# Two of the seven block additions of a fast matrix product moved from VectorE into TensorE's PSUM accumulation

## The chip, the cores and the metric

The kernel runs on one core of one Trainium2 chip. The metric is device time in microseconds (us) of one execution. A core has five engines that work side by side and hand over by semaphores: TensorE (PE in the profile, its weight loads PEld), VectorE (DVE), ScalarE (ACT), GpSimd (POOL) and SyncE (SP). TensorE writes only into PSUM, here eight banks of 512 float32 numbers for each of 128 partitions. VectorE and ScalarE read PSUM[...].

## The reference

A macaron block on 4 x 2048 tokens of width 256: half a mixture-of-experts layer, attention, and half a mixture-of-experts layer again, each on a layer norm and with a residual. Everything is float32.

```python
x = x + 0.5 * ffn(layernorm(x))      # 8 experts, top 2, capacity 1.25
x = x + attn(layernorm(x))
x = x + 0.5 * ffn(layernorm(x))

def ffn(x):                          # what matters here
    capacity = int(1.25 * N / E)     # 1280 rows for each of 8 experts
    disp = ...                       # each expert's rows, gathered
    g = einsum("ecd,edf->ecf", disp, wg)      # d = 256, f = 1024
    u = einsum("ecd,edf->ecf", disp, wu)
    eo = einsum("ecf,efd->ecd", silu(g) * u, wd)
    ...                              # weighted and added back to the rows
```

## The kernel before

The two mixture layers are two calls of `experts`. The 1280 rows of an expert are worked in two **units** of 640 rows (`chunks`, five tiles of 128 rows), so a layer has 16 units and the kernel 32. `k` is the unit's number within its layer. A unit has two stages: gate and up (`steps_of`), then the down projection (L680) with the scatter of its rows.

**Gate and up.** The products with `wg` and `wu` are made by a seven-product scheme for 2 x 2 blocks (Strassen in Winograd's form): the width 256 is split into two halves of 128, the rows into two halves of BH = 320, the outputs f into two halves of 512. Sums of weight blocks (`ws`, `sums_of_w`) are made once for an expert, sums of row blocks (`xs`, `sums_of_x`) once for a unit, by VectorE. A unit has NF = 4 **blocks**, p = 0 to 3, of 128 output columns in each half. A block makes seven products, each a pair of matmuls of 128 x 128 by 128 x 320, m = 0 for gate and m = 1 for up. In the order of the code they are: the *first* (`first_product`, weights block 11 with row block 11), the *second* (`p2`), the *third* (into `u2`, L577), the *sixth* (into `ct[:, 3]`, L578), the *fourth* (into `ct[:, 2]`, L580), the *fifth* (`p5`, L583) and the *seventh* (into `ct[:, 1]`, L590). Seven additions on VectorE, all recorded on the helper's line L487, put them together in `ct`, which holds four quarters of gate and up. Then ScalarE takes SiLU of the gate quarters (L563) and the product of gate and up goes to `h` (L566): on GpSimd in one piece for p < 3, on VectorE in two pieces for the last block, where ScalarE works a quarter at a time.

**PSUM.** `banks()` (L515) gives a buffer `mm` of two banks, three of them in turn; `both` fills one with a pair, gate in the first bank and up in the second. The first product alone is made in a single-bank buffer `one` (L547), gate and up at different places of the order, and ScalarE copies each half to `p1` in SBUF (L551), since two additions need it. The seventh and eighth bank are `one` and `tr` (transposes). The down projection's sums also take `banks()`.

**Order.** In `experts` the order on TensorE, VectorE and ScalarE is the order of the source (`tc.manual_schedule(engines=ENGINES - {Pool})`); GpSimd's is planned by the framework, and SyncE only issues large loads. Each engine works its own list in order, and the framework adds the semaphore waits that the tiles' readers and writers need. Between blocks, `beside(k, p)` puts in work for the next unit: after block 1 ScalarE masks three gathered row tiles (`blank`, L470), after block 2 two more; after blocks 2 and 3 TensorE transposes row tiles (L481), which ScalarE copies out (L484). During the down projection `behind(k, i)` adds the remaining transposes, the row and weight sums, the list of the next expert's rows, and the gathers on GpSimd's queue.

The first unit of a layer (k = 0) starts before all its rows have come: its first and second products need only the first 320 rows, and `rest_of_first` (L517) masks, transposes and sums the rest before the third.

Of the kernel before, what the change touches and what calls it, by code (L numbers as in the profile page):

```python
# [8 lines left out]
F32 = mybir.dt.float32  # L9
# [3 lines left out]
AF = mybir.ActivationFunctionType  # L13
ALU = mybir.AluOpType
# [4 lines left out]
P = 128  # L19
# [7 lines left out]
def macaron_kernel(  # L27
# [22 lines left out]
    nc = tc.nc  # L50
# [9 lines left out]
    BANK = 512  # L60
# [374 lines left out]
    BH = CH * P // 2  # L435
    TURN = 3

    def experts(name, src, dst, wait_for, weights, wpool, pool, ppool):
# [23 lines left out]
        def blank(k, *tiles):  # L462
            for i in tiles:
                if k < len(chunks):
                    e, r = chunks[k][0], got[k][i]
                    has = r[:, D + E + e : D + E + e + 1]
                    if k == 0 and i % 2:
                        nc.vector.tensor_scalar(r[:, 0:D], r[:, 0:D], has, None, ALU.mult)
                    else:
                        nc.scalar.mul(r[:, 0:D], r[:, 0:D], has)  # L470

        def turn(k, q):

            if k >= len(chunks):
                return
            if q == 0:
                turned[k] = xTs[k] = pool.tile([P, DC, CH * P], F32, tag="xsT", name="xsT", bufs=2)
            c, i0, i1 = q // 2, (0, TURN)[q % 2], (TURN, CH)[q % 2]
            ps = ppool.tile([P, BANK], F32, tag="tr", name="tr", bufs=1)
            for i in range(i0, i1):  # L480
                nc.tensor.transpose(  # L481
                    ps[:, (i - i0) * P : (i - i0 + 1) * P], got[k][i][:, c * P : (c + 1) * P], ident
                )
            nc.scalar.copy(turned[k][:, c, i0 * P : i1 * P], ps[:, : (i1 - i0) * P])  # L484

        def tt(o, a, b, op):
            nc.vector.tensor_tensor(o, a, b, op)  # L487
# [14 lines left out]
        def sums_of_x(k):  # L502
            if k >= len(chunks):
                return
            v = turned.pop(k)
            o = xs[k] = pool.tile([P, 4, BH], F32, tag="xs", name="xs", bufs=1)
            b11, b12, b21, b22 = v[:, 0, :BH], v[:, 0, BH:], v[:, 1, :BH], v[:, 1, BH:]
            tt(o[:, 0, :], b12, b11, ALU.subtract)
            tt(o[:, 1, :], b22, o[:, 0, :], ALU.subtract)
            tt(o[:, 2, :], b22, b12, ALU.subtract)  # L510
            tt(o[:, 3, :], b21, o[:, 1, :], ALU.subtract)

        def banks():

            return ppool.tile([P, 2, BANK], F32, tag="mm", name="mm", bufs=3)  # L515

        def rest_of_first():  # L517

            blank(0, *range(TURN, CH))
            for q in (1, 3):  # L520
                turn(0, q)
            sums_of_x(0)

        def steps_of(k):
            e = chunks[k][0]
            xT, hs = xTs.pop(k), []

            def product(p, m, ps, j, c, b):

                if c is None:  # L530
                    a = ws[e][:, m, j, p * P : (p + 1) * P]
                else:
                    a = weights[e][m][:, c, j * FH + p * P : j * FH + (p + 1) * P]
                nc.tensor.matmul(ps, a, b, start=True, stop=True)  # L534

            def both(p, *what):
                ps = banks()
                for m in range(2):
                    product(p, m, ps[:, m, :BH], *what)
                return ps[:, :, :BH]  # L540

            p1 = {}

            def first_product(p, m):
                if p == NF:
                    return
                one = ppool.tile([P, BANK], F32, tag="one", name="one", bufs=1)  # L547
                product(p, m, one[:, :BH], 0, 0, xT[:, 0, :BH])
                if m == 0:
                    p1[p] = pool.tile([P, 2, BH], F32, tag="p1", name="p1", bufs=2)  # L550
                nc.scalar.copy(p1[p][:, m, :], one[:, :BH])  # L551

            first_product(0, 0)
            for p in range(NF):
                last = p == NF - 1

                ct = pool.tile([P, 4, 2, BH], F32, tag="ct", name="ct", bufs=2)
                u2 = pool.tile([P, 2, BH], F32, tag="u2", name="u2", bufs=1)
                h = pool.tile([P, 2, CH * P], F32, tag="h", name="h", bufs=NF)
                hq = h.rearrange("p j (t s) -> p (j t) s", t=2)  # L560

                def silu(qs):
                    nc.scalar.activation(ct[:, qs, 0, :], ct[:, qs, 0, :], AF.Silu)  # L563

                def finish(engine, qs):
                    engine.tensor_tensor(hq[:, qs, :], ct[:, qs, 0, :], ct[:, qs, 1, :], ALU.mult)  # L566

                p2 = both(p, 0, 1, xT[:, 1, :BH])
                if p == 0:
                    first_product(0, 1)  # L570
                    if k == 0:
                        rest_of_first()
                    x4 = xs.pop(k)
                tt(ct[:, 0], p1[p], p2, ALU.add)
                if last:
                    silu(slice(0, 1))
                tt(u2, p1.pop(p), both(p, 1, None, x4[:, 1, :]), ALU.add)  # L577
                tt(ct[:, 3], u2, both(p, 2, None, x4[:, 2, :]), ALU.add)  # L578
                first_product(p + 1, 0)
                tt(ct[:, 2], ct[:, 3], both(p, 1, 1, x4[:, 3, :]), ALU.add)  # L580
                if last:
                    silu(slice(2, 3))
                p5 = both(p, 0, None, x4[:, 0, :])  # L583
                tt(ct[:, 1], u2, p5, ALU.add)
                tt(ct[:, 3], ct[:, 3], p5, ALU.add)
                first_product(p + 1, 1)
                if last:
                    silu(slice(3, 4))
                    finish(nc.vector, slice(0, 4, 2))
                tt(ct[:, 1], ct[:, 1], both(p, 3, None, xT[:, 1, BH:]), ALU.add)  # L590
                if last:
                    silu(slice(1, 2))
                    finish(nc.vector, slice(1, 4, 2))
                else:
                    silu(slice(0, 4))
                    finish(nc.gpsimd, slice(0, 4))
                hs.append(h)
                yield hs
# [54 lines left out]
        first = following[0]  # L653
        with tc.manual_schedule(engines=ENGINES - {mybir.EngineType.Pool}):
# [14 lines left out]
            for k, (e, i0) in enumerate(chunks):  # L669
                for p, hs in enumerate(steps_of(k)):  # L670
                    beside(k, p)
# [4 lines left out]
                for i, p, j in order:  # L676
                    if i not in po:
# [4 lines left out]
                        start=(p == 0 and j == 0), stop=(p == NF - 1 and j == 1),  # L682
# [399 lines left out]
    with tc.tile_pool(name="w1", bufs=2) as wpool:  # L1082
        weights = {}
        with tc.tile_pool(name="r1", bufs=1) as pool, tc.tile_pool(name="r1p", bufs=2, space=PSUM) as ppool:
# [5 lines left out]
            with tc.manual_schedule(engines=ENGINES):  # L1090
                nc.gpsimd.memset(wrx, 0.0)
                ps = ppool.tile([P, DC, P], F32, tag="turn", name="wrT", bufs=1)
# [4 lines left out]
                ps = ppool.tile([P, DC, P], F32, tag="turn", name="means", bufs=1)  # L1097
# [74 lines left out]
```

## Time and profile before

| what | value |
|---|---|
| time, median of 3 runs | 2045.0 us (2043.48 to 2046.27) |
| the profiled execution | 2038.74 us, its span 2036.9 us, mean granted clock of TensorE 0.959 |
| TensorE busy (PE) | 1875.8 us, 92% |
| weight loads (PEld) | 1440.3 us, 71% |
| VectorE busy | 1417.6 us, 70% |
| ScalarE busy | 657.1 us, 32% |
| GpSimd busy | 883.1 us, 43% |
| additions of products on VectorE (L487 with `mm`) | 896, some 820 ns each |
| ScalarE copies of the first product (L551) | 256, 427 ns each |
| SiLU on ScalarE (L563) | 224, 1.27 us for 1280 elements, 0.47 us for 320 |

A page gives busy time by engine, the span in 40 slices, and groups of instructions by line with the mean length of one and the idle time of its engine before them. A float32 matmul of the source stands as two matmul instructions and two weight loads. Records of successive matmuls overlap[...].

The two mixture layers stand at about 105 to 914 us and 1213 to 2037 us of the span; the attention lies between them, and a router with little work for TensorE ahead of each layer.

### The profile page before, as it was taken

The page shows a single profiled execution, that of the slowest core. Times are in us where ns is not written, and L with a number is a line of the kernel's source. Part 1 is how long each engine was busy: PE and PEld are TensorE (multiplying, and loading weights), DVE is VectorE, ACT ScalarE, POOL GpSimd, SP SyncE. Part 2 cuts the span into 40 slices and gives each one's busy share as a digit, 9 for nine tenths or more (in the row PEclk, how much of TensorE's full clock was granted, in tenths as well). Part 3 has the DMA queues.
Part 4 walks back from the last instruction along what each step waited for, and adds up shares of the span by engine and source line. Part 5 has one row for each costly group of instructions (what it writes and reads, how often), then busy time and mean ns, then how long its engine had stood idle before and what let it go on. Part 6 is the DMA issues. An engine that isn't in the chain of part 4 may idle for free.

```text
span 2036.9 us, 24719 instructions
## 1 busy us (share of the span) xinstructions
PE 1875.8 (92%) x9176; PEld 1440.3 (71%) x9176; DVE 1417.6 (70%) x2531; ACT 657.1 (32%) x1325; POOL 883.1 (43%) x737
## 2 busy tenths in 40 slices
PE   6379999999999999998999528999999999999998
PEld 4247777777777777777887415777777777777776
DVE  8867676767676767546798886767676676767654
ACT  5322323232223223225565403232222222232221
POOL 5335353535353535335555303535353535353533
PEclk8589999999999999999999858999999999999999
DMA  9902222223131322115002631313232313131211
GB/s 349 302 28 38 78 40 77 57 59 78 38 80 37 79 40 41 17 16 171 32 32 86 206 111 28 79 37 79 39 82 37 82 37 82 35 85 34 43 14 14
DMA packets 99928, 147.63 MB, mean 72 GB/s; under 512 B 7512, under 2 KB 86368, under 8 KB 99680
## 3 DMA queue, kind: packets, MB, share of 16 engines
q1 hardware_dynamic: 69072, 102.77, 15.0%
q0 software_dynamic: 30720, 43.27, 12.9%
q8 instruction: 73, 1.20, 0.3%
q14 instruction: 47, 0.39, 0.1%
q10 hardware_dynamic: 16, 0.01, 0.0%
HBM read 98.84 MB, written 55.57 MB: 76 GB/s over the span
## 4 chain that ended last, share of the span: by engine, by line
PE 83%; DVE 5%; issue 4%; ACT 1%; POOL 1%; DMA 1%; POOLq 0%; DVEq 0%; ACTq 0%; SPq 0%
PE mm L534 41%; PE mm L680 27%; PE one L534 7%; PE tr L481 2%; PE qp L804 1%; PE pc L859 1%; PE ix L404 1%; PE py L917 1%; DVE st L929 1%; DVE xw L927 1%; DVE q L812 1%; DVE m L817 0%; DVE z L826 0%; DVE st L788 0%; PE trq L847 0%
## 5 line engine op out<-in xcount | busy, mean ns | idle before, releaser
L680 PE MATMUL mm<-wdt,h 128*128 128x256 f32 x2560 | 579.0, 381 | 0.0
L680 PEld LDWEIGHTS mm<-wdt,h 128*128 128x128 f32 x2560 | 475.9, 190 | 63.9
L566 POOL TENSOR_TENSOR h<-ct 128x1280 f32<-128x1280 f32 x96 | 279.0, 2906 | 420.2 <-ACT ct L563 417.6
L534 PE MATMUL mm<-xs,ws 128*128 128x320 f32 x1536 | 456.9, 434 | 2.0 <-DVE xs L487 2.0
L534 PEld LDWEIGHTS mm<-xs,ws 128*128 128x128 f32 x1536 | 292.6, 191 | 124.3 <-DVE xs L487 2.5
L487 DVE TENSOR_TENSOR ct<-ct,mm 128x640 f32<-128x640 f32 x384 | 314.4, 819 | 89.4 <-PE mm L534 83.4
L487 DVE TENSOR_TENSOR ct<-p,mm 128x640 f32<-128x640 f32 x128 | 105.1, 821 | 243.4 <-ACT p L551 200.5
L563 ACT ACTIVATE ct<-ct 128x320 f32<-128x320 f32 (+1 forms) x224 | 182.2, 814 | 278.5 <-DVE ct L487 278.5
L487 DVE TENSOR_TENSOR ct<-u,mm 128x640 f32<-128x640 f32 x256 | 210.3, 822 | 61.1 <-PE mm L534 58.0
L551 ACT COPY p<-one 128x320 f32<-128x320 f32 x256 | 109.3, 427 | 405.4 <-PE one L534 404.4
L690 POOL DMA_INDIRECT out_dram<-eo,ixs x80 | 133.1, 1664 | 220.7 <-ACT eo L689 213.7
L690 POOL DMA_INDIRECT acc<-eo,ixs x80 | 132.8, 1660 | 221.2 <-ACT eo L689 214.2
L456 POOL DMA_INDIRECT r<-rows,ixs x160 | 159.0, 994 | 145.0 <-issue 106.5
L689 ACT ACTIVATE eo<-mm,r 128x256 f32<-128x256 f32 x160 | 76.2, 476 | 396.0 <-PE mm L680 396.0
L534 PE MATMUL mm<-xsT,ws 128*128 128x320 f32 x512 | 158.7, 432 | 0.0
L395 DVE TENSOR_TENSOR lo<-count,slot_lo 128x1024 f16<-128x1024 int16 x112 | 128.3, 1220 | 0.0
L534 PEld LDWEIGHTS mm<-xsT,ws 128*128 128x128 f32 x512 | 97.3, 190 | 40.5
L487 DVE TENSOR_TENSOR u<-p,mm 128x640 f32<-128x640 f32 x128 | 104.9, 820 | 17.0 <-PE mm L534 17.0
L534 PE MATMUL mm<-xsT,wgt 128*128 128x320 f32 x256 | 91.0, 437 | 0.0
L534 PE MATMUL one<-xsT,wgt 128*128 128x320 f32 x256 | 91.0, 437 | 0.0
L534 PE MATMUL mm<-xsT,wut 128*128 128x320 f32 x256 | 90.4, 435 | 0.0
L534 PE MATMUL one<-xsT,wut 128*128 128x320 f32 x256 | 89.9, 433 | 0.0
(209 smaller groups left out, 2316.4 us busy)
## 6 DMA issues: line engine op xcount, KB each, us to landing
wgt<-in_L_ffn_wg_dram SPq DMA_DIRECT2D x16, 1024.0 KB, 4.9
wut<-in_L_ffn_wu_dram SPq DMA_DIRECT2D x16, 1024.0 KB, 6.9
wdt<-in_L_ffn_wd_dram SPq DMA_DIRECT2D x16, 1024.0 KB, 5.5
rows<-xw SPq DMA_DIRECT2D x7, 2176.0 KB, 11.8
xw<-in_L_attn_x_dram SPq DMA_DIRECT2D x16, 512.0 KB, 8.8
out_dram<-xw SPq DMA_DIRECT2D x16, 512.0 KB, 2.9
xw<-acc SPq DMA_DIRECT2D x15, 512.0 KB, 8.7
r<-rows,ixs POOLq DMA_INDIRECT x160, 2.8
```

The source lines that it names most:

```text
L395: nc.vector.tensor_tensor(lo, spread(count.unsqueeze(1), shape), spread(at.unsqueeze(2), shape), ALU.is_equal)
L404: nc.tensor.matmul(self.ps[q, :], self.hv[:, t, :, :], lo[:, t % TG, :], start=(t < Q), stop=(t >= T - Q),)
L456: nc.gpsimd.indirect_dma_start(out=r, out_offset=None, in_=src[:, :], in_offset=bass.IndirectOffsetOnAxis(ap=lists[e][:, i : i + 1], axis=0),)
L481: nc.tensor.transpose(ps[:, (i - i0) * P : (i - i0 + 1) * P], got[k][i][:, c * P : (c + 1) * P], ident)
L487: nc.vector.tensor_tensor(o, a, b, op)
L534: nc.tensor.matmul(ps, a, b, start=True, stop=True)
L551: nc.scalar.copy(p1[p][:, m, :], one[:, :BH])
L563: nc.scalar.activation(ct[:, qs, 0, :], ct[:, qs, 0, :], AF.Silu)
L566: engine.tensor_tensor(hq[:, qs, :], ct[:, qs, 0, :], ct[:, qs, 1, :], ALU.mult)
L680: nc.tensor.matmul(po[i], hs[p][:, j, i * P : (i + 1) * P], weights[e][2][:, j * NF + p, :], start=(p == 0 and j == 0), stop=(p == NF - 1 ...
L689: nc.scalar.mul(eo, po[i], got[k][i][:, D + e : D + e + 1])
L690: ins = nc.gpsimd.indirect_dma_start(out=dst[:, :], out_offset=bass.IndirectOffsetOnAxis(ap=lists[e][:, i0 + i : i0 + i + 1], axis=0), in_ ...
```

## The change

Two additions go into TensorE's accumulation. A matmul with `start=False` adds to what stands in its banks in place of overwriting it.

- The first product's pair is now made in one two-bank buffer of `banks()`, gate and up one after the other, each followed by its copy to `p1`. The second product is then added onto it in the same banks (`onto`, `second_product`), and ScalarE takes the sum out directly: SiLU of the gate half into `ct[:, 0, 0]`, a copy of the up half into `ct[:, 0, 1]`. The addition into `ct[:, 0]` is gone, in all blocks.
- In blocks 0 to 2 the seventh product is added onto the fifth in the fifth's banks, after VectorE has read the fifth for `ct[:, 3]`. One addition makes `ct[:, 1]` from `u2` and the sum. The last block keeps its two additions.
- The first product of block p + 1 stands between the fifth and the seventh of block p. In block 0 the first product stands at the beginning of the unit and, for k > 0, the second behind the third. For k = 0 the second product stands ahead of `rest_of_first`, and with it ScalarE's SiLU.
- The SiLU at the end of blocks 0 to 2 takes three quarters (960 elements) in place of four. The buffer `one` is left to the row lists.

So a block's order on TensorE for p > 0 becomes: second, third, sixth, fourth, fifth, first of the next block, seventh.

```diff
@@ -525,13 +525,14 @@
             e = chunks[k][0]
             xT, hs = xTs.pop(k), []
 
-            def product(p, m, ps, j, c, b):
+            def product(p, m, ps, j, c, b, start=True):
+
 
                 if c is None:
                     a = ws[e][:, m, j, p * P : (p + 1) * P]
                 else:
                     a = weights[e][m][:, c, j * FH + p * P : j * FH + (p + 1) * P]
-                nc.tensor.matmul(ps, a, b, start=True, stop=True)
+                nc.tensor.matmul(ps, a, b, start=start, stop=True, skip_group_check=not start)
 
             def both(p, *what):
                 ps = banks()
@@ -539,18 +540,24 @@
                     product(p, m, ps[:, m, :BH], *what)
                 return ps[:, :, :BH]
 
-            p1 = {}
-
-            def first_product(p, m):
+            first = {}
+
+            def first_product(p):
+
                 if p == NF:
                     return
-                one = ppool.tile([P, BANK], F32, tag="one", name="one", bufs=1)
-                product(p, m, one[:, :BH], 0, 0, xT[:, 0, :BH])
-                if m == 0:
-                    p1[p] = pool.tile([P, 2, BH], F32, tag="p1", name="p1", bufs=2)
-                nc.scalar.copy(p1[p][:, m, :], one[:, :BH])
-
-            first_product(0, 0)
+                ps = first[p] = banks()
+                p1 = pool.tile([P, 2, BH], F32, tag="p1", name="p1", bufs=2)
+                for m in range(2):
+                    product(p, m, ps[:, m, :BH], 0, 0, xT[:, 0, :BH])
+                    nc.scalar.copy(p1[:, m, :], ps[:, m, :BH])
+                first[p] = ps, p1
+
+            def onto(p, ps, *what):
+                for m in range(2):
+                    product(p, m, ps[:, m, :BH], *what, start=False)
+                return ps[:, :, :BH]
+
             for p in range(NF):
                 last = p == NF - 1
 
@@ -565,34 +572,41 @@
                 def finish(engine, qs):
                     engine.tensor_tensor(hq[:, qs, :], ct[:, qs, 0, :], ct[:, qs, 1, :], ALU.mult)
 
-                p2 = both(p, 0, 1, xT[:, 1, :BH])
+                def second_product(ps):
+                    c11 = onto(p, ps, 0, 1, xT[:, 1, :BH])
+                    nc.scalar.activation(ct[:, 0, 0, :], c11[:, 0, :], AF.Silu)
+                    nc.scalar.copy(ct[:, 0, 1, :], c11[:, 1, :])
+
                 if p == 0:
-                    first_product(0, 1)
-                    if k == 0:
-                        rest_of_first()
+                    first_product(0)
+                ps, p1 = first.pop(p)
+                if k == 0 and p == 0:
+                    second_product(ps)
+                    rest_of_first()
+                elif p > 0:
+                    second_product(ps)
+                if p == 0:
                     x4 = xs.pop(k)
-                tt(ct[:, 0], p1[p], p2, ALU.add)
-                if last:
-                    silu(slice(0, 1))
-                tt(u2, p1.pop(p), both(p, 1, None, x4[:, 1, :]), ALU.add)
+                tt(u2, p1, both(p, 1, None, x4[:, 1, :]), ALU.add)
+                if p == 0 and k > 0:
+                    second_product(ps)
                 tt(ct[:, 3], u2, both(p, 2, None, x4[:, 2, :]), ALU.add)
-                first_product(p + 1, 0)
                 tt(ct[:, 2], ct[:, 3], both(p, 1, 1, x4[:, 3, :]), ALU.add)
                 if last:
                     silu(slice(2, 3))
                 p5 = both(p, 0, None, x4[:, 0, :])
-                tt(ct[:, 1], u2, p5, ALU.add)
                 tt(ct[:, 3], ct[:, 3], p5, ALU.add)
-                first_product(p + 1, 1)
                 if last:
+                    tt(ct[:, 1], u2, p5, ALU.add)
                     silu(slice(3, 4))
                     finish(nc.vector, slice(0, 4, 2))
-                tt(ct[:, 1], ct[:, 1], both(p, 3, None, xT[:, 1, BH:]), ALU.add)
-                if last:
+                    tt(ct[:, 1], ct[:, 1], both(p, 3, None, xT[:, 1, BH:]), ALU.add)
                     silu(slice(1, 2))
                     finish(nc.vector, slice(1, 4, 2))
                 else:
-                    silu(slice(0, 4))
+                    first_product(p + 1)
+                    tt(ct[:, 1], u2, onto(p, p5, 3, None, xT[:, 1, BH:]), ALU.add)
+                    silu(slice(1, 4))
                     finish(nc.gpsimd, slice(0, 4))
                 hs.append(h)
                 yield hs
```

## The prediction

> **What bounds the kernel now.** I read the stage table first (busy time of each engine in stretches of 50 us, columns PE, PEld, DVE, ACT, POOL, granted clock, DMA share, GB/s). One row of each kind:
>
> ```profile
> 0.00:50.00 50.00, 30.62 (x406) 24.19 (x406) 40.66 (x147) 26.51 (x70) 29.55 (x66) 0.89 1.01 337
> ...
> 700.00:750.00 50.00, 50.00 (x209) 38.40 (x208) 31.78 (x44) 15.33 (x31) 19.33 (x10) 1.00 0.31 79
> 750.00:800.00 50.00, 50.00 (x266) 37.57 (x265) 37.46 (x47) 15.04 (x30) 25.56 (x18) 1.00 0.21 39
> ...
> 1150.00:1200.00 50.00, 6.46 (x61) 4.55 (x62) 42.77 (x192) 10.41 (x22) 4.29 (x12) 0.55 0.63 218
> ```
>
> From 150 to 900 us and from 1250 to 2000 us every row has PE busy 50.00 of 50 at clock 1.00. These are the two feed-forward stages, where the whole change lies. VectorE is busy 32 to 38 of 50 there, ScalarE about 15. A busy matmul row can hide waiting, so I checked the groups and the timeline:
>
> ```profile
> L534 PE MATMUL mm<-xs,ws 128*128 128x320 f32 x1536 | 456.9, 434 | 2.0 <-DVE xs L487 2.0
> L487 DVE TENSOR_TENSOR ct<-ct,mm 128x640 f32<-128x640 f32 x384 | 314.4, 819 | 89.4 <-PE mm L534 83.4
> L551 ACT COPY p<-one 128x320 f32<-128x320 f32 x256 | 109.3, 427 | 405.4 <-PE one L534 404.4
> ```
>
> ```profile
> 738.80 2.32 PE L534 MATMUL mm<-xs,ws 128*128 128x320 f32 x8
> 740.95 0.70 PE L534 MATMUL one<-xsT,wgt 128*128 128x320 f32 x2
> 741.49 0.70 PE L534 MATMUL mm<-xs,wgt 128*128 128x320 f32 x2
> 742.03 0.70 PE L534 MATMUL mm<-xs,wut 128*128 128x320 f32 x2
> ```
>
> The last column of the groups is idle time before them: 2.0 us in 1536 matmul instructions, while VectorE and ScalarE wait for the matmuls. In the timeline (start, length, engine) one matmul of the source is two instructions and starts 0.54 us after the one before, always. A block p has 14, so 14 x 0.54 = 7.5 us; its seven additions take 7 x 0.82 = 5.7 us beside it. TensorE alone sets the pace, without slack.
>
> **What the Trainium skill says.** "PSUM — Partial Sum Buffer", section "PSUM bank collisions raise a hardware error", wants semaphores by bank and quadrant: two engines may work in different banks at once. The trace agrees: VectorE reads one pair of banks while TensorE fills the next. So no hardware rule makes the second matmul of a pair wait for a reader of the first one's bank; only the program's own waits can. "ScalarE: Activation LUTs", section "What ACT_TABLE_LOAD costs", gives 186 ns + 0.833 ns per element, 93 ns overlap of neighbours, and 1283 ns for a table load. The trace has 427 ns for 320 elements (453 by the formula) and 1.28 us for the load, and I use those. "TensorE: Matmul & The Clock Gate", section "What's actually happening", halves the clock only after an idle window of some 3.4 us. The trace has clock 1.00 at 1000 us with PE busy 48.93 of 50, and 0.55 where PE is busy 6.46. I charge nothing for the clock in mid-stage.
>
> **The change part by part.**
>
> *Additions removed.* 7 x 128 = 896 additions become 96 x 5 + 32 x 6 = 672. The 224 that go, some 0.82 us each, take 184 us off VectorE. All of it lies beside matmuls: worth 0, since TensorE's count stays at 14 per block. The POOL product may start a little earlier; nothing waits for it. Its reader, the down projection, starts several us later.
>
> *ScalarE's new work.* 128 times a SiLU (0.47 us) and a copy (0.43 us) out of the product's banks; against it 96 SiLUs shrink from 1280 to 960 elements (1.27 to about 1.00 us, by line through 0.47 at 320) and 32 go. Sum 128 x 0.90 - 96 x 0.27 - 32 x 0.47 = +74 us, ScalarE from 32% to 36%. By itself it costs nothing.
>
> *The pair of first products.* Here I expect the loss. Before, the two matmuls of a first product stand apart, each in its own allocation of `one`, with other products between. Now they stand next to each other in one two-bank buffer, and ScalarE's copy of the first half is recorded between them. In the order of the built program the second matmul of every pair (128 of 128) carries a wait on ScalarE, and by its count it is for the copy of the first half of the same buffer: the reader of one bank holds the writer of the other. TensorE works in order, so everything behind stands too.
>
> Its price from rows of before. A pair `one` starts at 740.95; its copy on ScalarE starts at 741.69, so 0.74 after the start of the matmul, and takes 0.43:
>
> ```profile
> 738.78 1.27 ACT L563 ACTIVATE ct<-ct 128x1280 f32<-128x1280 f32 x1 [1.50 <-DVE ct L487]
> 739.96 1.30 ACT L470 ACTIVATE r<-r 128x256 f32<-128x256 f32 x3
> 741.69 0.43 ACT L551 COPY p<-one 128x320 f32<-128x320 f32 x1 [0.44 <-PE one L534]
> ```
>
> From a release to running matmuls, the start of the stage shows both steps (127.67 + 0.49 = 128.16 against a weight load at 128.22; three instructions take 1.08 us from a standstill and 0.97 in a stream at 133.98):
>
> ```profile
> 127.67 0.49 DVE L487 TENSOR_TENSOR xs<-xsT,xs 128x320 f32<-128x320 f32 x1 [0.41 <-ACT xsT L484]
> ...
> 128.22 1.08 PE L534 MATMUL mm<-xs,ws 128*128 128x320 f32 x3 [0.99 <-DVE xs L487]
> ```
>
> So 0.74 + 0.43 + 0.05 + 0.11 = 1.33 us from the first matmul to the second, where 0.54 would do: 0.79 us lost per pair. Four pairs per unit, 32 units, less the two that open a stage: 126 x 0.79 = **99.5 us**. Bounds: 0.70 and 0.90, so 88 to 113 us. Nothing covers it.
>
> *Seventh product onto the fifth.* It waits until VectorE has read the fifth. That read starts 0.20 after the fifth's slot ends, takes 0.82, and with 0.16 to restart frees TensorE at 1.18; the first-product pair in between takes 1.08 + 0.79 = 1.87. Hidden, 0. Without the stall above it would show 0.10 us, 96 times.
>
> *Second product onto the first.* It waits for the copy of the second half: 0.79 after that half's slot, covered by the 1.08 of the product between them (the seventh; in block 0 the third). 0.
>
> *Banks held longer.* The first product's pair stays taken until ScalarE has read the sum. By the built order the fourth product takes those banks in block 1, due 6 x 0.54 = 3.23 us after the block's second product began; in blocks 0, 2 and 3 it is the fifth (due at 8 x 0.54 = 4.30 in block 2). In block 2 ScalarE does ahead of that: the SiLU of block 1 from 1.12 (0.20 + 0.82 + 0.10 after the seventh) for 1.00 less 0.09 overlap, three maskings of 0.405 apart, SiLU 0.47 less 0.09, copy 0.43; it ends at 4.05, and TensorE runs at 4.21. It fits by 0.09. Block 1 fits by 0.24, block 3 by 0.46. Charged 0; the upper bound is 0.3 us in block 2 of 30 units, 9 us.
>
> *Opening of each stage (k = 0).* Copy, copy, table load, SiLU and copy now stand ahead of the masking of the last gathered rows, on which the x sums and then TensorE wait. Before, the load stood here, off the path:
>
> ```profile
> 134.35 1.28 ACT L563 ACT_TABLE_LOAD   x1
> ```
>
> The masking began at 125.43 in the first stage. Following the chain at the half clock of that stretch (first half copied by 123.40, second by about 124.9, load to 126.2, SiLU and copy to 127.0) it begins 1.5 to 2.2 us later; at most one clock window later still. I take 2 us per stage, **4 us**, bounds 2 and 8. DMA queues, gathers and scatters keep their order: 0.
>
> Sum 99.5 + 4 = +103.5 us. The profiled execution, 2038.74 us (span 2036.9), becomes 2142; it lies 6.3 us under the median of 2045.0, to which I add the same: **2148 us**.
>
> **The rivals.**
> - *Stall absent*: the wait is met before TensorE arrives. Then the seventh's 0.10 x 96 = 10 us and the 4 us of the openings stay: 2059 us. For it: the banks differ. Against it: ScalarE cannot copy before the first matmul has ended, 0.2 us after the second should have begun.
> - *Banks as well*: ScalarE's reading late in blocks 2 and 3, behind maskings, and the row copy adds some 0.8 us in both: 30 x 1.6 = 48 us more, 2196 us. Against it: those blocks take banks that VectorE frees, until the fifth product.
> - *Faster*: VectorE's release of banks paces the stage and the even matmul rows hide it. The 184 us of additions would then be worth up to all of themselves, 1861 us at the lowest. It decides once a block's VectorE work exceeds 7.5 us; it is 5.7, and VectorE is the one that waits (89.4 us before one group). The same cause at a tiny size would give no change.
>
> **Numbers.** A measurement of this kernel tells about 0.2%, 4 us, from no change. Stall as worked out: 0.86; banks as well: 0.06; stall absent: 0.04 (slower too); VectorE pacing: 0.02 faster, and 0.02 no change. So slower 0.96, same 0.02, faster 0.02. The range takes the stall's bounds and the 9 us of block 2 and the openings: 2045 + 88 + 2 = 2135 to 2045 + 113 + 9 + 8 = 2175, and a little below for stalls that a busier overlap shortens: 2125 to 2175.
>
> **What would show it.** In the profile after: idle time of TensorE before the second matmul of the first pair (`mm<-xsT,wut`), released by the copy into `p1`. The record of a pair's first half ends 0.70 us after its start, not 0.54, and the next may start with the weight load at 1.22, so only some 0.52 of the 0.79 shows as idle: 66 us in all, and PE busy near 48 of 50 in the feed-forward rows. The sure sign is the length of a block, 8.3 us in place of 7.5; VectorE near 1230 us; clock still 1.00. I am wrong if that group has no idle time, if idle time stands instead before the fourth or fifth product with the copy into `ct` as releaser, or if the rows still read 50.00.

## The result and the profile after

The changed kernel takes **2159.24 us** (median of 4 runs, 2158.96 to 2159.46) against 2045.01 us: 1.0559 times the time of before, 95% interval 1.0541 to 1.0577, or 114 us more. The forecast was 2148 us, in a range of 2125 to 2175. The profiled execution has a span of 2157.0 us against 2036.9, so 120.1 us more; the execution profiled before lay 6.3 us under its own median, this one at its median.

The stage table of `after`, the rows that answer to those of before (columns as there):

```profile
700.00:750.00 50.00, 47.88 (x250) 34.08 (x249) 29.22 (x36) 14.84 (x33) 26.13 (x17) 1.00 0.22 40
750.00:800.00 50.00, 47.88 (x197) 35.38 (x195) 23.81 (x34) 15.93 (x36) 16.42 (x9) 1.00 0.29 78
```

TensorE, busy 50.00 of 50 before, now stands 2 us in each 50, at full clock. VectorE has become lighter, 1245.4 us in place of 1417.6 over the whole, and that bought nothing. Whom TensorE waits for is in the list of waits (who waits, for whom: us in total, times, longest) and in the group of the second matmul of a pair:

```profile
PEld mm L535 <- ACT p L553: 133.6, 128, 1.4
PE mm L535 <- ACT p L553: 67.7, 128, 0.6
PEld mm L535 <- DVE u L487: 24.1, 60, 0.4
```

```profile
L535 PE MATMUL mm<-xsT,wut 128*128 128x320 f32 x512 | 195.3, 464 | 67.7 <-ACT p L553 66.7
```

Two releasers are new: ScalarE's copy of the first product (128 times) and VectorE's addition into `u2` (60 times). Neither total is the loss itself. A weight load counts its idle time from the load before, so its total is too large. The record of a matmul runs on after the next one may start (0.70 us below, where the next is due after 0.54), so the idle time behind it, and with it the other total, is too small. What is lost is read from the starts. The timeline of `after`, around one pair (start, length):

```profile
724.52 0.70 PE L535 MATMUL mm<-xsT,wgt 128*128 128x320 f32 x2
...
725.26 0.43 ACT L553 COPY p<-mm 128x320 f32<-128x320 f32 x1 [2.96 <-PE mm L535]
...
725.74 0.81 PE L535 MATMUL mm<-xsT,wut 128*128 128x320 f32 x2 [0.52 <-ACT p L553]
...
726.38 1.24 PE L535 MATMUL mm<-xsT,ws 128*128 128x320 f32 x4
```

From the gate half at 724.52 to the seventh product behind the pair at 726.38 are 1.86 us, where two matmuls take 1.08: 0.78 lost, as the copy begins 0.74 after the gate half and holds the up half until it ends. And in block 2, the other wait:

```profile
738.24 0.82 DVE L487 TENSOR_TENSOR u<-p,mm 128x640 f32<-128x640 f32 x1 [1.39 <-PE mm L535]
...
739.12 0.81 PE L535 MATMUL mm<-xs,wgt 128*128 128x320 f32 x2
```

The fourth product takes the banks of the third. VectorE has read those at 738.24 + 0.82 = 739.06, which is also when the fourth product's first matmul should run. Its weights are released at 739.12 and the matmul can run at about 739.22, so that the next one starts at 739.76, one matmul of 0.54 later. That is 0.16 us lost.

A unit's gate and up, from the first matmul of its first product to the first of its down projection, shows the sum. Rows of the timelines, before and then after:

```profile
721.57 0.70 PE L534 MATMUL one<-xsT,wgt 128*128 128x320 f32 x2
...
752.27 6.21 PE L680 MATMUL mm<-wdt,h 128*128 128x256 f32 x28
```

```profile
717.28 0.70 PE L535 MATMUL mm<-xsT,wgt 128*128 128x320 f32 x2
...
751.48 5.78 PE L694 MATMUL mm<-wdt,h 128*128 128x256 f32 x26
```

30.70 us became 34.20. The down projection kept its 17.82 or 20.02 us. All 32 units, from the same starts:

| units | number | gate and up before | after | more, in all |
|---|---|---|---|---|
| first of each layer | 2 | 35.20 and 37.31 | 44.35 and 43.31 | 15.2 us |
| ordinary | 28 | 30.70 | 34.20 | 98.0 us |
| last of each layer | 2 | 30.15 | 33.33 | 6.4 us |

That is 119.6 of the 120.1 us. The last units have no fourth product that waits for VectorE, so their 3.18 us is the four pairs alone, some 0.79 each. An ordinary unit's 3.50 is the same 3.18 and 0.32 for the fourth product in two blocks.

### The profile page after: what moved, and what is told of

Its sections match the earlier page's. It is cut to its first block, busy times and chain, and to the rows that moved or that the text cites. A ratio compares the mean times of both kernels' runs of the same rounds, so it can differ in the third digit from the quotient of the medians.

```text
span 2157.0 us, 24808 instructions
## 1 busy us (share of the span) xinstructions
PE 1926.4 (89%) x9176; PEld 1426.7 (66%) x9176; DVE 1245.4 (58%) x2307; ACT 703.6 (33%) x1549; POOL 883.6 (41%) x737
## 4 chain that ended last, share of the span: by engine, by line
PE 80%; DVE 5%; issue 5%; ACT 4%; POOL 1%; DMA 1%; POOLq 0%; ACTq 0%; DVEq 0%; SPq 0%
PE mm L535 47%; PE mm L694 25%; ACT p L553 3%; PE tr L481 2%; PE qp L818 1%; PE pc L873 1%; PE ix L404 1%; PE py L931 1%; DVE st L943 1%; DVE xw L941 1%; DVE q L826 1%; DVE m L831 0%; DVE z L840 0%; DVE st L802 0%; PE trq L861 0%
## 5 line engine op out<-in xcount | busy, mean ns | idle before, releaser
L535 PE MATMUL mm<-xs,ws 128*128 128x320 f32 x1536 | 464.4, 435 | 2.0 <-DVE xs L487 2.0
L487 DVE TENSOR_TENSOR ct<-ct,mm 128x640 f32<-128x640 f32 x288 | 236.3, 821 | 79.5 <-PE mm L535 77.8
L535 PE MATMUL mm<-xsT,wut 128*128 128x320 f32 x512 | 195.3, 464 | 67.7 <-ACT p L553 66.7
L553 ACT COPY p<-mm 128x320 f32<-128x320 f32 x256 | 109.1, 426 | 415.2 <-PE mm L535 401.6
L570 ACT ACTIVATE ct<-ct 128x960 f32<-128x960 f32 (+1 forms) x192 | 141.4, 736 | 284.0 <-DVE ct L487 284.0
L535 PEld LDWEIGHTS mm<-xsT,wut 128*128 128x128 f32 x512 | 87.7, 191 | 154.3 <-ACT p L553 130.7
L535 PE MATMUL mm<-xsT,wgt 128*128 128x320 f32 x512 | 182.3, 438 | 1.0 <-ACT p L553 1.0
L535 PEld LDWEIGHTS mm<-xsT,wgt 128*128 128x128 f32 x512 | 94.4, 192 | 35.2 <-ACT p L553 2.9
L535 PE MATMUL mm<-xs,wgt 128*128 128x320 f32 x256 | 96.6, 459 | 0.0
```

The lines of the kernel that those rows point to most:

```text
L535: nc.tensor.matmul(ps, a, b, start=start, stop=True, skip_group_check=not start)
L553: nc.scalar.copy(p1[:, m, :], ps[:, m, :BH])
```

## The experiments

The theory: the wait of a pair's second matmul for the copy of its first half costs 0.79 us 128 times. Rivals: the banks held longer or the accumulation itself cost the time; or the seventh product's wait for the fifth does. Each edit is against the changed kernel unless it says otherwise. The kernel before ran beside every group of runs, with medians of 2040.8 to 2044.8 us, so ratios to it are the safer comparison between groups.

**1. Both matmuls ahead of the copies.**

```diff
                 for m in range(2):
                     product(p, m, ps[:, m, :BH], 0, 0, xT[:, 0, :BH])
-                    nc.scalar.copy(p1[:, m, :], ps[:, m, :BH])
+                for m in range(2):
+                    nc.scalar.copy(p1[:, m, :], ps[:, m, :BH])
```

> Both matmuls of a first-product pair are issued before the two copies of it; nothing else differs from the changed kernel. Theory (the second matmul of the pair waits for ScalarE's copy of the first half, 0.79 us, 128 times): that wait is gone, -101 us. The seventh product then reaches the fifth's banks 1.08 us after the fifth and waits for VectorE's read, 0.10 to 0.17 us in 96 blocks, +10 to 16 us; the fourth product's wait in blocks 2 and 3 stays. About 2071 us. Rival A (banks held longer, or accumulation itself, cost the time): hardly any change, 2150 to 2160 us. Rival B (the seventh's wait on the fifth costs the time): no gain, 2155 us or more.

Measured 2073.09 us, ratio 1.0145 (1.0125 to 1.0165); the changed kernel has 1.0559. The pair's wait is gone and the next ones show in the list of waits of this run:

```profile
PEld mm L535 <- DVE ct L487: 35.7, 93, 1.4
PEld mm L535 <- DVE u L487: 24.0, 60, 0.4
```

The first is the seventh product waiting for the fifth to be read, the second the fourth product as before. An ordinary unit takes mostly 31.36 us, 0.66 over the 30.70: twice 0.16 for the fourth and three times 0.11 for the seventh. Most of the loss was the place of one copy.

**2. One of the two additions only: the second product.** The seventh gets banks and an addition of its own again.

```diff
-                    tt(ct[:, 1], u2, onto(p, p5, 3, None, xT[:, 1, BH:]), ALU.add)
+                    tt(ct[:, 1], ct[:, 1], both(p, 3, None, xT[:, 1, BH:]), ALU.add)
```

(with `tt(ct[:, 1], u2, p5, ALU.add)` ahead of `first_product(p + 1)`)

> Only the second product goes onto the first, the seventh has banks and an addition of its own as in the kernel before (in all blocks). Theory: the pair's wait is all here, and the seventh's part is hidden behind it, so the time stays at 2159 us, within 4 us. Rival B (seventh onto fifth is the loss): back to 2045 to 2060 us. Rival A (banks): in between or slower, since the seventh takes one more pair of banks, 2160 to 2190 us.

Measured 2159.80 us, ratio 1.0582 (1.0564 to 1.0600), ordinary units 34.23 us. The whole loss is in this half of the change; the seventh onto the fifth costs nothing as long as the pair's wait stands between them.

**3. The other addition only**, on the kernel before: the first product keeps its single bank.

```diff
-                tt(ct[:, 1], u2, p5, ALU.add)
                 tt(ct[:, 3], ct[:, 3], p5, ALU.add)
                 first_product(p + 1, 1)
...
-                tt(ct[:, 1], ct[:, 1], both(p, 3, None, xT[:, 1, BH:]), ALU.add)
+                tt(ct[:, 1], u2, onto(p, p5, 3, None, xT[:, 1, BH:]), ALU.add)
```

(the last block unchanged)

> The kernel before, with the seventh product put onto the fifth in blocks 0 to 2 as the only edit; the first product stays in its single bank, its halves apart. Only one matmul of the first product (0.54 us) now stands between the fifth and the seventh, while the fifth is free again 1.18 to 1.25 us after its end. Theory: 0.64 to 0.71 us of wait in 96 blocks, 61 to 68 us: about 2109 us. Rival (the accumulation is hidden wherever it stands): 2045 us. Rival B (it is the whole loss): 2150 us.

Measured 2106.62 us, ratio 1.0319 (1.0302 to 1.0337). The timeline of this run shows the wait between the one matmul behind the fifth and the seventh:

```profile
703.47 1.24 PE L534 MATMUL mm<-xs,ws 128*128 128x320 f32 x4
704.55 0.70 PE L534 MATMUL one<-xsT,wut 128*128 128x320 f32 x2
705.62 1.34 PE L534 MATMUL mm<-xsT,ws 128*128 128x320 f32 x4 [0.38 <-issue]
```

The seventh was due at 704.55 + 0.54 = 705.09 and the product behind it starts at 706.80 where 706.17 was due: 0.63 us, three times a unit; most units take 32.62 us, 1.92 more. So an addition that is free in one order costs 0.6 us in another. By their ratios the two halves of the change cost 5.8% and 3.2% alone and 5.6% together: in the changed order the pair's wait stands between the fifth and the seventh, and covers the seventh's.

**4. The suspected wait made longer.**

```diff
+                again = pool.tile([P, BH], F32, tag="again", name="again", bufs=1)
                 for m in range(2):
                     product(p, m, ps[:, m, :BH], 0, 0, xT[:, 0, :BH])
+                    if m == 0:
+                        nc.scalar.copy(again, ps[:, m, :BH])
                     nc.scalar.copy(p1[:, m, :], ps[:, m, :BH])
```

> The changed kernel with the copy of the first half made twice (once more into a scratch tile) ahead of the second matmul of the pair. Theory: the wait grows by one more copy in a row, 0.34 us (0.43 less 0.09 overlap), 128 times, 44 us: about 2203 us. If the wait were met by other work, or ended by something else than this copy: 2159 us.

Measured 2205.84 us, ratio 1.0807 (1.0789 to 1.0825), 46.6 us over the changed kernel. The second matmul of the pair now waits through both copies:

```profile
742.39 0.81 PE L535 MATMUL mm<-xsT,wut 128*128 128x320 f32 x2 [0.90 <-ACT again L555]
```

Its idle time is 0.90 us where the changed kernel has 0.52, and ordinary units take 35.62 to 35.68 us, some 1.45 more than there: 0.36 for each of the four pairs, near the 0.34 that was forecast. So TensorE follows the length of ScalarE's copying.

**5. The second product behind the third in all blocks.** The pair stays as it is.

```diff
-                elif p > 0:
-                    second_product(ps)
...
-                if p == 0 and k > 0:
+                if p > 0 or k > 0:
                     second_product(ps)
```

> The changed kernel, except that in blocks 1 to 3 too the second product stands behind the third (as it does in block 0). The pair's wait of 0.79 us stays. Theory: the fourth product's wait in blocks 2 and 3 of 30 units (0.17 us each, for VectorE's reading of the third) goes, since the second product now stands between: 10 us faster than the changed kernel, 2149 us. Rival (banks read out late by ScalarE behind its maskings): the fifth product then waits in block 2, slower than 2159 us.

Measured 2149.30 us, ratio 1.0536 (1.0520 to 1.0552). The interval overlaps that of the changed kernel, and by the ratios the gain is 0.23%, half of the 10 us that were forecast. The trace decides: ordinary units take 33.88 us, 0.32 less than 34.20 and alike in all 28, 9 us together, and in the list of waits of this run the row of VectorE's `u` is gone; the pair's is left:

```profile
PEld mm L535 <- ACT p L553: 136.5, 130, 1.5
```

**6. The opening of a layer.** In the first unit the second product moves behind the third.

```diff
                 if k == 0 and p == 0:
-                    second_product(ps)
                     rest_of_first()
...
-                if p == 0 and k > 0:
+                if p == 0:
                     second_product(ps)
```

> The changed kernel, except that in the first unit of a layer the second product (with ScalarE's SiLU and copy) stands behind the third as in the other units, no longer ahead of the masking of the last rows. The first units of the two layers took 9.15 and 6.0 us more than before in gate and up, of which 2.7 each are the known waits; 9.7 us are left. Theory (the chain copy, copy, sum, SiLU, copy ahead of the masking, at half clock): most of it goes, less the second product's own 1 to 2 us per layer, which now stands on the path: 5 to 8 us faster than the changed kernel, 2151 to 2154 us. Rival (the opening is late for another reason, or it is only the clock's window): within 2 us of 2159.

Measured 2155.66 us, ratio 1.0562 (1.0546 to 1.0578). By the ratio there is no gain, so the forecast of 5 to 8 us is not met in the total. By the trace the two first units take 41.0 and 40.9 us in place of 44.35 and 43.31, so 5.8 us went there; the stretches ahead of the first layer and between the layers, which differ by some us from run to run, took 2.2 more. The place of the second product explains 5.8 of the 9.8 us that the openings lost beside the known waits (worked out below); the total does not show it.

**7. Everything mended, with one addition and with two.** One copy of 640 elements behind both matmuls, the second product behind the third everywhere; in the first kernel the seventh apart, in the second onto the fifth, which is issued ahead of the fourth:

```diff
-                tt(ct[:, 3], u2, both(p, 2, None, x4[:, 2, :]), ALU.add)
-                tt(ct[:, 2], ct[:, 3], both(p, 1, 1, x4[:, 3, :]), ALU.add)
+                tt(ct[:, 2], u2, both(p, 2, None, x4[:, 2, :]), ALU.add)
                 p5 = both(p, 0, None, x4[:, 0, :])
-                tt(ct[:, 3], ct[:, 3], p5, ALU.add)
+                tt(ct[:, 3], ct[:, 2], p5, ALU.add)
+                tt(ct[:, 2], ct[:, 2], both(p, 1, 1, x4[:, 3, :]), ALU.add)
```

> Only the second product goes onto the first: both matmuls of the pair are issued before one copy of 640 elements, and the second stands behind the third in all blocks and in the first unit; the seventh has its own banks and addition. Theory: every wait of a block is covered, only the openings differ, so this equals the kernel before within 0.2% (0 to 4 us more), though VectorE has 128 additions fewer. If fewer additions were worth anything by themselves, it would be faster than before by more than 0.3%.

> Both additions by TensorE, with the pair, its one copy and the second product as in second_mended, and the fifth product issued ahead of the fourth (VectorE keeps u2 plus sixth in ct's third quarter, so that the fifth is read first). Between fifth and seventh stand then 2.15 us of matmuls against 1.25 us until its banks are free. Theory: no wait is left in a block; time of the kernel before within 0.2% (0 to 4 us more), with 224 additions fewer on VectorE. Rival (the seventh's wait can't be covered, or the fourth then waits for ScalarE's reading of the second): 10 to 20 us more than before.

Measured 2045.42 us for both, ratios 1.0023 (1.0013 to 1.0033) and 1.0023 (1.0014 to 1.0031). The stage table of the second:

```profile
700.00:750.00 50.00, 50.00 (x211) 38.41 (x210) 25.53 (x36) 16.19 (x33) 17.84 (x9) 1.00 0.31 79
750.00:800.00 50.00, 50.00 (x264) 37.44 (x263) 32.41 (x40) 15.75 (x33) 26.24 (x17) 1.00 0.22 39
```

TensorE is full again, ordinary units take 30.70 us as before, with 224 additions fewer on VectorE. So in the blocks the accumulation itself costs nothing, no bank is short, and the lighter VectorE is worth nothing. By the medians 4.6 us stay, a little over the 4 of the forecast. In the traces the openings, 38.1 and 38.0 us, are together 3.6 us longer than before; the rest was not traced to a place.

**8. The openings.** On `fifth_early`, the masking of the last rows ahead of the pair's copy; then also idle matmuls while the first rows are gathered; at last these alone on the kernel before.

```diff
                     product(p, m, ps[:, m, :BH], 0, 0, xT[:, 0, :BH])
+                ahead_of_copy()             # rest_of_first where k == 0
                 nc.scalar.copy(p1, ps[:, :, :BH])
...
-            for q in (0, 2):
-                turn(0, q)
+            stay_busy(banks()[:, 0, :], 8)
+            turn(0, 0)
+            stay_busy(banks()[:, 0, :], 1, 256)
+            turn(0, 2)
```

> fifth_early, with one edit in the first unit of each layer: the masking, transposes and sums of the last rows are recorded right behind the two matmuls of the first pair, ahead of ScalarE's copy of that pair. The blocks of all other units already take the time of before in fifth_early, so what is left is in these two openings. Theory: the masking no longer waits for the pair at half clock and the copy, so the third product starts about 1 us earlier per layer: 2 us less than fifth_early, within 0.15% of the kernel before. Rival (the gathers or the clock window set the opening): same as fifth_early, 0.2% over before.

> masks_first, with eight idle matmuls of 512 columns on TensorE while the first rows are being gathered, and one of 256 columns between the first two groups of transposes; their results are not used. Theory: the granted clock of TensorE is 0.5 through the openings, since it was idle before them; with work in that stretch it is full when the first pair starts, which then takes 1.1 us in place of 2.1, as do the third and second behind it: 3 to 5 us less per layer than fifth_early, 2 to 6 us below the kernel before in all (0.1 to 0.3%). Rival: the clock does not hold through the sparse transposes, or the idle matmuls delay the first transpose: no gain over masks_first, or up to 3 us more.

> The kernel before with the idle matmuls of kept_warm in the two openings as the only edit. If kept_warm owes its time to the clock in the openings alone, this gains the same 0.2 to 0.3% (4 to 6 us) on before, and the additions moved to TensorE are worth nothing in either direction. Rival (VectorE's 224 additions fewer help once the waits are gone): this gains less than 0.1%.

Measured: 2043.64 us, ratio 0.9998 (0.9990 to 1.0006); 2038.89 us, 0.9972 (0.9962 to 0.9983); 2039.45 us, 0.9982 (0.9972 to 0.9992). Stretches of the opening in the stage table, first of `after`, then of `kept_warm` (third column from the right: granted clock):

```profile
120.00:130.00 10.00, 7.02 (x14) 3.26 (x14) 0.35 (x1) 4.56 (x9) 4.81 (x6) 0.50 0.30 86
130.00:140.00 10.00, 8.68 (x20) 5.26 (x20) 4.97 (x8) 0.62 (x3) 0.00 (x0) 0.62 0.01 2
```

```profile
120.00:130.00 10.00, 7.49 (x30) 4.77 (x30) 3.81 (x7) 5.32 (x10) 5.67 (x6) 1.00 0.37 99
130.00:140.00 10.00, 10.00 (x38) 7.10 (x38) 5.75 (x7) 2.45 (x4) 2.90 (x1) 1.00 0.00 0
```

In `kept_warm` the idle matmuls hold the clock at 1.00, and it is the one version with both additions moved that is faster than before, by 0.28% (0.17 to 0.38). But the same edit on the kernel before gains 0.18% (0.08 to 0.28), and the two intervals overlap. Since the idle matmuls are the only edit there, that gain is theirs; that all of it comes through the clock was not shown. A gain or a loss from the moved additions is not shown.

The traces hold more than these totals. In `masks_first` the first units take 34.7 and 34.5 us, some 3.5 a layer less than in `fifth_early`, where 1 was forecast: in the first layer the clock is at 1.00 from 130 to 140 us, where `fifth_early` has 0.82 on average. But 14 of its 28 ordinary units, and 13 in `kept_warm`, take about 31.0 us or more in place of 30.70. The sum over all ordinary units is 5.9 and 4.9 us. A new row of the list of waits of `kept_warm` shows TensorE waiting for VectorE:

```profile
PEld mm L535 <- DVE ct L487: 10.1, 23, 0.9
```

`fifth_early` has the same order of products and no such row; why it came stays open. So `kept_warm` (first units 33.3 and 33.3) and `before_warm` (36.1 and 34.4, ordinary units 1.8 over) come to nearly the same time in different ways, and whether `kept_warm` without this wait would beat `before_warm` was not tried.

## Why the prediction was right, and where it was off

**The pairs.** Forecast 0.79 us, 126 times, 99.5 us, the two pairs that open a layer apart. In the ordinary and last units, and three times in each first unit, the trace shows that sum. Experiments 1, 2 and 4 took the wait away, found it in one half of the change, and lengthened it, each within 4 us of the forecast made for it. This step was right in place, mechanism and size. That ScalarE reads one bank while TensorE would write the other, which the Trainium skill's "PSUM — Partial Sum Buffer" (section "PSUM bank collisions raise a hardware error") allows, made no difference: the second matmul of the pair waited for the copy all the same. No run here lets the two banks of one buffer be used so, or gives each half of the pair a buffer of its own, so that remedy is not shown.

**Additions removed, ScalarE's new work, accumulation: 0.** Right; experiment 7 has all three and full TensorE rows. ScalarE went from 657.1 to 703.6 us, less than the +74 of the sum.

**Seventh onto fifth: 0 behind the pair, 0.10 us without it.** Right: `second_only` and the changed kernel take the same, and 0.11 us shows in `two_copies`, once the pair's wait is gone.

**Banks held longer: 0, at most 9 us from ScalarE in block 2.** The size is near, the step is wrong. I worked out ScalarE's readers of the banks and took the fourth product's wait for VectorE's reading of the third as met. It is not: in block 2 above, that reading ends at 739.06, when the matmul should already start. By the numbers of the prediction itself the third is read, and TensorE running again, at 2 x 1.08 + 0.20 + 0.82 + 0.16 = 3.34 us, and the fourth is due at 3.23, a wait of 0.11. The trace has 0.16 us, 60 times: 10 us. No fifth product waited for ScalarE, though the margin was forecast at 0.09 us.

**Opening: 4 us, bounds 2 and 8.** Mis-sized: 15.2 us less the six pairs (4.7) and four fourth products (0.7) leave 9.8 us in the profiled executions, over the upper bound. In the first layer the masking began not 1.5 to 2.2 us later but 3.2, at 128.60 in place of 125.43. In the timelines of `before` and then of `after`:

```profile
125.43 0.51 ACT L470 ACTIVATE r<-r 128x256 f32<-128x256 f32 x1
```

```profile
125.39 1.28 ACT L577 ACT_TABLE_LOAD   x1
125.42 1.44 PE L535 MATMUL mm<-xsT,wgt 128*128 128x320 f32 x2 [0.52 <-ACT p L553]
...
127.96 0.44 ACT L577 ACTIVATE ct<-mm 128x320 f32<-128x320 f32 x1 [1.29 <-PE mm L535]
...
128.60 0.52 ACT L470 ACTIVATE r<-r 128x256 f32<-128x256 f32 x1
```

The table load is over at 126.67 and hides behind TensorE; the SiLU waits for the second product, at half clock until 127.92. The prediction's chain let the SiLU follow the load at 126.2, which leaves time for one matmul of the second product at half clock. It started only when both had ended, behind a copy that itself came 0.5 us later than forecast (125.38 in place of 124.9): this chain is the term that was too small. The clock, which before rose at 123.9, rose only at about 137.6, more than the one clock window that the prediction allowed for, so that the four matmuls (eight instructions) of the third and sixth products ran at half rate too. These are the rows of the stage table of `before` for the stretches shown above for `after`:

```profile
120.00:130.00 10.00, 7.16 (x23) 4.50 (x24) 3.17 (x7) 2.97 (x7) 4.76 (x6) 0.81 0.31 88
130.00:140.00 10.00, 10.00 (x39) 7.07 (x38) 7.09 (x10) 3.84 (x5) 2.80 (x1) 1.00 0.00 0
```

Where the clock is 0.5 and then 1.00, a mean of 0.81 puts the rise at 123.8, and the 0.62 of `after` puts it at 137.6.

**Sum.** 103.5 forecast, 120.1 between the two profiled executions: 10 from the fourth product and 6 from the openings. Against the medians, 114.2, the miss is 11 us, since the execution profiled before was itself 6.3 us faster than its median. Of the rivals, *banks as well* names a real kind of wait, with the wrong engine and about five times its size (48 us, where 10 were found); *stall absent* and *faster* fell.

## What to carry to other kernels

Work taken off an engine with slack was worth nothing here, and what has to be checked is which waits the new order adds to the engine without slack: one copy recorded between two matmuls of one buffer cost 100 us, and with both matmuls recorded ahead of it that wait was gone. Before putting a product onto another in place, count the time until its bank has been read (about 1.2 us here) against the matmuls issued in between, and find every product whose banks that shift moves behind another reader. A buffer of two banks was one thing to the program's waits here.

## What was not expected of the hardware

The granted clock at a layer's opening depends on how much TensorE works there: nine idle matmuls, the only edit between `masks_first` and `kept_warm`, kept it at 1.00 from 120 us on, where `masks_first` has 0.66 from 120 to 130 us. The pauses of 0.5 us in the pair are not the whole of it: `two_copies` has none, and its clock is still at 0.50 from 120 to 130 us and 0.70 from 130 to 140. Nor is the edit always enough: in `before_warm` the clock fell to 0.50 from 128.4 to 131.8 us. The Trainium skill ("TensorE: Matmul & The Clock Gate", section "What's actually happening") says that the clock rises after a busy window of some 3.4 us and falls after an idle one, and that these windows do not start anew with a kernel. The traces agree in length: in `before` the clock is 1.00 from 110.2 to 113.6 us and 0.50 from there to 123.9, one and three times 3.4. That the spread of the kernel before, 2038.9 to 2046.9 us in one group of runs, comes from such windows is likely but was not shown. In mid-stage, pauses of 0.8 us in every 8 left the clock at 1.00 throughout.
